# Half-size weight pieces, the second weight's extremes moved behind the first quantization, row moments by batch-norm statistics, and two halves stored from ScalarE's queue, in a block of involution and ternary convolutions

## Chip, cores and metric

One core of one Trainium2 chip. The metric is the device time of one execution in microseconds (us), as a median of runs. Data are f32; the convolutions multiply f32 data that were rounded to fp32r and their remainders.

## The reference, cut to what matters

Input x is (8, 256, 56, 56). Layer 0 is an involution on the group-normalized x, layer 1 two ternary convolutions with batch norm:

```python
x = x + involution(group_norm(x), w_reduce, b_reduce, w_span, b_span)   # K = 7, 16 groups
h = group_norm(x)
out1 = relu(batch_norm(tri_conv(h, w1)))          # 3x3, 256 -> 256
x = x + relu(out1 + batch_norm(tri_conv(out1, w2)))

def tri_conv(x, w):
    tw = w - mean(w)                              # mean of the whole weight
    lo = min(tw) + (max(tw) - min(tw)) / 3
    hi = max(tw) - (max(tw) - min(tw)) / 3
    tq = -1 where tw < lo, 1 where tw > hi, else 0
    return conv3x3(x, tq) + conv1x1(x, tq[:, :, 1, 1])
```

So each weight (256 x 256 x 3 x 3) needs its sum, maximum and minimum over all of it before any element can be made ternary, and each batch norm needs sums and sums of squares over all images before the next layer can begin.

## The kernel before, in words

**Stage 1, the involution (to about 1150 us).** An image is four quarters of 64 channels, a quarter ten rows of tiles, so the main loop (L940 to L988) has 8 x 4 x 10 = 320 rows. In a row, TensorE (PE) multiplies the row's patches with the matrices of its quarter (`apply_row`, L815), transposes the patches of later rows (L749) and makes some of the 14 units of the next quarter's matrices (`generate`, L782). VectorE (DVE) and ScalarE (ACT) move the units out of PSUM (L791, L786); ACT, DVE and GpSimd (POOL) take the result to x (`pick_out`, L827, L828, L831). POOL spreads normalized strips of x into `xn` (L674), PE transposes them (L717), ACT copies them to `stg` (L720), SyncE's queue (SP) stores them in `xtd` (L708) and loads patches `q` from there four rows ahead (L742). `params` (L557) makes the next image's group norm in steps, two a row from row 20 of each image. `pin` (L864) chains each engine's instructions in the order of the text, so in this stage every engine works in that order.

**Before the main loop** x of image 0 is loaded by halves of a quarter (L545). Then SP issues the loads of both whole weights into `wf` (L631, four DMAs of 1152 KB) and after them 16 stores of zeros from `xn` into the borders of `xtd` (L637); POOL may write `xn` only when these have read it. `extremes` (L195) takes each weight in QM = 6 pieces of 768 columns: DVE finds maximum and minimum (L208, L209), ACT the sum (L210, written over the piece itself). Nine of these 12 steps stand in the three `reduce` steps at L902 to L906 (PE's `pk`, L651; ACT's `kr`, L656), the rest in the loop over the first quarter's 14 units (L908). There too stand, for each weight, the steps that combine partitions: DVE L213 to L218, PE matmul and transpose `ends` (L222, L223), DVE L225 to L227, PE `all` (L230), DVE L232 to L245.

**Quantization** runs beside the rows from row 8, one step of the generator `quant` a row (L984). Each weight is 16 pieces of 3 x 96 columns and seven steps (rows) a piece: load into the one `piece` buffer (L257), two rows later the two comparisons (L261, L262), then L264, L273 (in half of the pieces) and L277, then L279 to L281, then L283 and L284, which leave six planes of 96 columns. The store of the planes (L287) is put into `tasks` and issued by `transfer(2)` near the head of the next row. 32 pieces make 224 rows.

**Stages 2 and 3, the convolutions** (`conv_phase`, L315): 16 halves of images, each six groups of 24 x 2 matmuls (`ORDER`, L464). From a group's results DVE makes four rows of y in turn (L484, L450). ACT takes sums and sums of squares of a half (L416, one pass each) while the next half runs (`statistics`); for the last half, `last_rows` (L420) does it row by row: rows 1 and 2 after group 4, row 0 after group 0, row 3 after group 5. Each half is stored by SP's queue, the last by ACT's (L504). `batch_norm_params` (L175) adds the columns of the statistics up (L177) and makes scale `sc` and offset `bi`, for which the next stage waits. In these stages the framework may order instructions otherwise than the text does.

**Stage 4** (L1052): loads of y1, y2, x1 (L1060), two passes each by ACT and DVE, and a store by ACT's queue (L1065).

Of the kernel before, what the change touches and what calls it, by code (L numbers as in the profile page):

```python
# [2 lines left out]

# [5 lines left out]
F32 = mybir.dt.float32  # L9
# [8 lines left out]
P = 128  # L18
# [60 lines left out]

QN, QJ = 96, 3 * C // 96
QS = WT
SLOT = (0, 2, 3, 4, 5, 1)
QM = 6


@with_exitstack
def involution_tri_block_kernel(
# [20 lines left out]
    def const_tile(shape, name):  # L110
        return const.tile(shape, F32, tag=name, name=name)
# [9 lines left out]
        for name, src in (("g1", g1), ("b1", b1), ("g2", g2), ("b2", b2)))  # L121


    st1, st2 = (const_tile([P, CT, 2, 2 * B + 2], name) for name in ("st1", "st2"))

    nc1, nc2 = (const_tile([P, CT], name) for name in ("nc1", "nc2"))
    mv2 = const_tile([P, B, NCQ, 2], "mv2")
# [62 lines left out]
        return sc, bi  # L190

    def piece_of(pool, name):
        return pool.tile([P, (4 + QS) * QN], F32, tag="piece", name=f"piece_{name}")

    def extremes(w, cols, pool, transposer, psum_tile, name):  # L195

        nf = CT * 9 * C
        n_cols = [3]

        def col(n=1):  # L200
            n_cols[0] += n
            return cols[:, n_cols[0] - n:n_cols[0]]

        s, mx, mn = col(QM), col(QM), col(QM)
        f = nf // QM
        for j in range(QM):
            v = w[:, j * f:(j + 1) * f]
            nc.vector.tensor_reduce(mx[:, j:j + 1], v, AX.X, ALU.max)  # L208
            nc.vector.tensor_reduce(mn[:, j:j + 1], v, AX.X, ALU.min)  # L209
            nc.scalar.activation(v, v, AF.Identity, accum_out=s[:, j:j + 1])  # L210
            yield
        sums, ends = col(), col(2)
        nc.vector.tensor_reduce(sums, s, AX.X, ALU.add)  # L213
        nc.vector.tensor_reduce(ends[:, 0:1], mx, AX.X, ALU.max)
        nc.vector.tensor_reduce(ends[:, 1:2], mn, AX.X, ALU.min)
        nc.vector.tensor_scalar(ends[:, 1:2], ends[:, 1:2], -1.0, None, ALU.mult)
        v = piece_of(pool, name)
        nc.vector.memset(v[:, :P], 1.0)  # L218
        yield

        ps = psum_tile(f"ends_{name}")
        nc.tensor.matmul(ps[:, P:P + 1], v[:, :P], sums, start=True, stop=True)  # L222
        nc.tensor.transpose(ps[:2, :P], ends, transposer)  # L223
        mean, top = cols[:, 0:1], col()
        nc.vector.tensor_scalar(mean, ps[:, P:P + 1], 1.0 / (P * nf), None, ALU.mult)  # L225
        nc.vector.tensor_reduce(top[:2], ps[:2, :P], AX.X, ALU.max)
        nc.vector.tensor_copy(v[:2, P:2 * P], top[:2].to_broadcast([2, P]))  # L227
        yield
        ps = psum_tile(f"all_{name}")
        nc.tensor.transpose(ps[:, :2], v[:2, P:2 * P], transposer[:2, :2])  # L230
        ex = col(2)
        nc.vector.tensor_copy(ex, ps[:, :2])  # L232
        amx, amn = ex[:, 0:1], ex[:, 1:2]

        nc.vector.tensor_tensor(amx, amx, mean, ALU.subtract)
        nc.vector.tensor_scalar(amn, amn, -1.0, mean, ALU.mult, ALU.subtract)

        d, q0, r, th = (col() for _ in range(4))
        nc.vector.tensor_tensor(d, amx, amn, ALU.subtract)
        nc.vector.tensor_scalar(q0, d, 1.0 / 3.0, None, ALU.mult)  # L240
        nc.vector.scalar_tensor_tensor(r, q0, -2.0, d, ALU.mult, ALU.add)
        nc.vector.tensor_tensor(r, r, q0, ALU.subtract)
        nc.vector.scalar_tensor_tensor(th, r, 1.0 / 3.0, q0, ALU.mult, ALU.add)
        nc.vector.tensor_tensor(cols[:, 1:2], amn, th, ALU.add)
        nc.vector.tensor_tensor(cols[:, 2:3], amx, th, ALU.subtract)  # L245
        yield

    def quantize(dst, w_dram, cols, pool, tasks, name):


        mean, lo, hi = (cols[:, k:k + 1] for k in range(3))
        for t in range(CT):
            for j in range(QJ):
                v = piece_of(pool, name)
                w, u = v[:, :3 * QN], v[:, 3 * QN:]
                o = (t * QJ + j) * 3 * QN
                nc.sync.dma_start(w, w_dram[:, o:o + 3 * QN])  # L257
                yield
                yield
                g = u[:, :3 * QN]  # L260
                nc.vector.tensor_scalar(g, w, mean, hi, ALU.subtract, ALU.is_gt)  # L261
                nc.vector.tensor_scalar(w, w, mean, lo, ALU.subtract, ALU.is_lt)  # L262
                yield
                nc.vector.tensor_tensor(g, g, w, ALU.subtract)  # L264

                def part(x, k):
                    return x[:, k * QN:(k + 1) * QN]


                c0, c1 = max(C, j * QN) - j * QN, min(2 * C, (j + 1) * QN) - j * QN  # L270
                if c0 < c1:
                    g1 = part(u, 0)[:, c0:c1]
                    nc.vector.tensor_scalar(g1, g1, 2.0, None, ALU.mult)  # L273

                e, f = part(w, 0), part(w, 1)
                g1, g0, g2 = (part(u, k) for k in range(3))
                nc.vector.tensor_tensor(e, g0, g2, ALU.add)  # L277
                yield
                nc.vector.scalar_tensor_tensor(f, g2, 4.0, g0, ALU.mult, ALU.add)  # L279
                nc.vector.tensor_tensor(part(u, 3), e, g1, ALU.add)  # L280
                nc.vector.tensor_tensor(part(u, 4), e, g1, ALU.subtract)  # L281
                yield
                nc.vector.scalar_tensor_tensor(part(u, 5), g1, 2.0, f, ALU.mult, ALU.add)  # L283
                nc.vector.scalar_tensor_tensor(part(u, 6), g1, -2.0, f, ALU.mult, ALU.add)  # L284

                def store(u=u[:, QN:], o=t * 3 * C + j * QN):
                    nc.sync.dma_start(  # L287
                        bass.AP(dst[:].tensor, dst[:].offset + o,
                                [[QS * CT * 3 * C, P], [CT * 3 * C, QS], [1, QN]]), u)

                tasks.append(store)
                yield
                yield

    def weights(i, k):

# [18 lines left out]
    def conv_phase(i, begun, src_d, norm, stats, shift, dst_d, follow):  # L315
# [104 lines left out]
        def last_rows(n, y, k0, m):  # L420

            for _ in sums(n, [y[:, to].rearrange("p (r k) -> p r k", k=4 * W)
                              [:, :, k0 * W:(k0 + m) * W] for to in range(CT)]):
                pass

        done = iter(())
        nxt, begun = {}, ({}, None)
        for _ in transform(0, raws, nxt):
# [5 lines left out]
        for n in range(2 * B):  # L434
# [22 lines left out]
            for k in ORDER:  # L457
# [34 lines left out]
                elif k == 0:  # L492
                    row_of(0, m[0], 1.5, s, ALU.add)
                    if final:
                        last_rows(n + 1, y, 0, 1)
                elif k == 5:
                    row_of(3, m[5], 6.0, d, ALU.add)
                    if final:
                        last_rows(n + 2, y, 3, 1)
                next(steps, None)  # L500
            for _ in steps:
                pass
            for to in range(CT):
                (nc.scalar if final else nc.sync).dma_start(  # L504
                    dst_d[b][to][:, h * NH:(h + 1) * NH], y[:, to])
            done = statistics(n, y)
        return begun
# [10 lines left out]
    with ExitStack() as ph1:  # L518
# [38 lines left out]
        def params(b):  # L557
# [12 lines left out]
                nc.vector.tensor_scalar(edge[:, j], dst[:, :, 1], side_sb[:, j:j + 1], None, ALU.mult)  # L570
            prm[b], prm_edge[b] = dst, edge
            yield
            ps = ps_one(f"br_{b}")
            for c in range(NCQ):
                for i in range(2):
# [46 lines left out]
        xe = [fixed([P, NX, HQ, QX], f"xe{i}") for i in range(2)]  # L622
        for v in xe:
            nc.gpsimd.memset(v, 0.0)

        nf = CT * 9 * C
        wf = apool1.tile([P, A_COLS], F32, tag="a1", name="wf")
        for i, v in enumerate((w1, w2)):
            for j in range(2):
                o = j * nf // 2  # L630
                nc.sync.dma_start(wf[:, i * nf + o:i * nf + o + nf // 2], v[:, o:o + nf // 2])  # L631
        zero = xn.rearrange("p k r x -> p (k r x)")

        for d in (d for ds in xt_d for d in ds):
            for r0, n in ((0, PAD), (PAD + HH, HQ - PAD - HH)):
                e = n * QX * RP // P
                nc.sync.dma_start(  # L637
                    bass.AP(d[:].tensor, d[:].offset + r0 * QX * RP, [[e, P], [1, e]]), zero[:, :e])

        def reduce(b, py):  # L640

# [250 lines left out]
        for _ in params(0):  # L892
            pass
        strips, around = prep(0), surround(0, 0)
        a_next = matrices(0)
        thresholds = [pieces.tile([P, 32], F32, tag=f"cols{i}", name=f"cols{i}") for i in range(2)]
        ext = [extremes(wf[:, i * nf:(i + 1) * nf], thresholds[i], pieces, ident_sb, ps_one, f"w{i}")
               for i in range(2)]

        found = chain(*(islice(v, QM) for v in ext), *ext)  # L900

        for py in range(PY):  # L902
            next(strips)
            transfer(len(tasks))
            reduce(0, py)
            for _ in range(3):  # L906
                next(found)
        for u, _ in enumerate(generate(0, 0, a_next)):  # L908
            if u < 4 or u % 3 == 0 and u < 12:
# [23 lines left out]
        for k in rows[:QLEAD]:  # L933
            transpose_q(*k)
        pin()
        norm = iter(())
        quant = chain(*(quantize(wq_d[i], v, thresholds[i], pieces, tasks, f"w{i + 1}")
                        for i, v in enumerate((w1, w2))))
        last = None
        for m, (b, c) in enumerate(quarters):  # L940
            a = a_next
# [195 lines left out]
```

## Time and profile before

| | |
|---|---|
| time, median of 3 runs | 2258.8 us (2254.0, 2258.8, 2258.85) |
| the profiled execution's own time | 2269.48 us |
| its span | 2267.7 us |
| granted TensorE clock, mean | 0.924 |
| busy, share of the span | PE 82%, PE weight loads 76%, DVE 75%, ACT 56%, POOL 26% |

Busy times of the stages, from the windows of that execution (us):

| window | what | PE | DVE | ACT | DMA share |
|---|---|---|---|---|---|
| 0 to 24 | loads of x, first group norm | 1.72 | 11.68 | 1.49 | 0.88 |
| 24 to 47 | `reduce` steps and extremes | 17.41 | 16.16 | 9.40 | 0.49 |
| 47 to 79 | the first quarter's units | 24.03 | 20.23 | 15.70 | 0.33 |
| 1156 to 1585 | first convolution | 428.71 | 407.02 | 278.76 | 0.36 |
| 1585 to 1601 | to the second | 0.29 | 10.85 | 8.97 | 0.71 |
| 1601 to 2030 | second convolution | 428.02 | 406.71 | 282.05 | 0.34 |

A line of the timeline reads: start and length in us, engine, line, operation, out<-in with their shapes, xcount, and in brackets how long the engine sat idle before it and what ended that. A line of the windows: the window, its length, then the busy time (and count) of PE, PEld, DVE, ACT and POOL, then the granted clock, the DMA share and GB/s. A group's line that has three durations with slashes gives the shortest, median and longest in ns. In the waits, each line has the sum, the number and the longest wait in us. The span's 40 slices have about 56.7 us each.

### The profile page before, as it was taken

How to read it: one execution, taken by the hardware profiler on the slowest of the kernel's cores; microseconds unless marked ns; L12 is line 12 of the kernel's file. 1: busy time of each engine (PE TensorE's matmuls, PEld its weight loads, DVE VectorE, ACT ScalarE, POOL GpSimd, SP SyncE). 2: the span in 40 equal slices, each digit the busy share in tenths (PEclk: the TensorE clock that was granted, in tenths of full speed). 3: DMA queues.
4: the chain of work that ended last, by engine and by line, in shares of the span. 5: the costliest groups of instructions: out<-in, count | busy, mean ns of one | idle time of the engine just before them, and what ended most of it. 6: DMA issues, size and time to landing. Idle time of an engine off the chain costs nothing.

```text
span 2267.7 us, 72706 instructions
## 1 busy us (share of the span) xinstructions
PE 1866.4 (82%) x31088; PEld 1716.6 (76%) x31088; DVE 1706.7 (75%) x2906; ACT 1268.3 (56%) x2461; POOL 584.5 (26%) x1320
## 2 busy tenths in 40 slices
PE   4889899898998989999879999999799999970000
PEld 3778777777877877778779999999799999970000
DVE  6676857667585775655689999998999999975444
ACT  3555455455554645556446766665576666673434
POOL 2545546364563645546400000000000000000000
PEclk9899999999999999999989999999899999995555
DMA  6556646566474754645453333334333333369999
GB/s 211 154 157 181 199 131 206 147 192 189 131 221 120 225 164 138 197 119 160 138 206 116 129 134 140 119 116 161 133 138 117 116 116 116 116 255 401 410 430 403
DMA packets 156447, 411.24 MB, mean 181 GB/s; under 512 B 51550, under 2 KB 62172, under 8 KB 148444
## 3 DMA queue, kind: packets, MB, share of 16 engines
q1 hardware_dynamic: 150528, 376.56, 49.9%
q10 hardware_dynamic: 5596, 30.03, 3.2%
q8 instruction: 245, 4.01, 0.8%
q14 instruction: 78, 0.64, 0.1%
HBM read 264.05 MB, written 142.48 MB: 179 GB/s over the span
## 4 chain that ended last, share of the span: by engine, by line
PE 38%; DMA 7%; DVE 3%; ACT 1%; issue 1%; ACTq 0%; SPq 0%; POOL 0%; DVEq 0%
PE c L464 37%; DMA y1f<-y1d 3%; DMA x1f<-x1d 2%; DMA out_y<-x1f 1%; DVE x1f L1064 1%; DMA y2f<-y2d 1%; ACT dummy L416 1%; DVE y1f L1062 0%; ACT y1f L1061 0%; ACT y1f L1063 0%; PE pa L815 0%; PE ptq L749 0%; DVE q L346 0%; DVE r L366 0%; DVE u L373 0%
## 5 line engine op out<-in xcount | busy, mean ns | idle before, releaser
L464 PE MATMUL c<-pl,wq 128*128 128x392 f32 x4608 | 857.1, 348 | 20.2 <-ACT pl L351 20.2
L464 PEld LDWEIGHTS c<-pl,wq 128*128 128x128 f32 x4608 | 855.1, 189 | 22.0 <-ACT pl L351 20.7
L791 DVE TENSOR_TENSOR a<-pg,bt 126x756 f32<-126x756 f32 (+3 forms) x640 | 393.2, 656 | 192.7 <-ACT a L786 147.3
L782 PE MATMUL pg<-kr,wl 64*126 64x140 f32 (+1 forms) x6144 | 459.4, 294 | 14.3 <-DVE a L791 7.1
L782 PEld LDWEIGHTS pg<-kr,wl 64*126 64x126 f32 x6144 | 396.8, 196 | 66.4 <-issue 41.5
L815 PE MATMUL pa<-a,q 126*32 126x48 f32 x17920 | 273.2, 208 | 62.3 <-issue 38.5
L815 PEld LDWEIGHTS pa<-a,q 126*32 126x32 f32 x17920 | 223.1, 111 | 115.8 <-issue 53.4
L786 ACT ACTIVATE a<-pg,bt 126x126 f32<-126x126 f32 x768 | 243.3, 475 | 102.6 <-PE pg L782 102.4
L831 POOL TENSOR_TENSOR x<-x,inv 128x168 f32<-128x168 f32 x320 | 166.4, 520 | 438.5 <-DVE inv L828 375.5
L828 DVE SCALAR_TENSOR_TENSOR inv<-pa,half_sb,inv 128x168 f32<-128x168 f32 x320 | 117.1, 366 | 171.0 <-ACT inv L827 144.8
L351 ACT CAST pl<-r 128x812 fp32r<-128x812 f32 x192 | 162.5, 868 | 145.2 <-DVE r L346 126.9
L752 ACT COPY q<-ptq 126x384 f32<-126x384 f32 x320 | 138.2, 481 | 162.7 <-issue 96.2
L331 POOL MEMSET xp<- 128x116 f32 x32 | 6.3, 195 | 829.4 <-DVE a L346 829.4
L416 ACT ACTIVATE dummy<-y,nc 128x1568 f32<-128x1568 f32 (+2 forms) x144 | 210.1, 1459 | 5.3 <-DVE y L484 3.5
L674 POOL TENSOR_SCALAR xn<-x,gn 128x224 f32<-128x224 f32 (+2 forms) x384 | 179.1, 486 | 130.0 <-PE pt L717 70.8
L352 DVE TENSOR_TENSOR pl<-r,pl 128x812 fp32r<-128x812 f32 x192 | 187.2, 1002 | 28.2 <-ACT pl L351 27.0
L674 POOL TENSOR_SCALAR xe<-x,gn 128x168 f32<-128x168 f32 (+2 forms) x384 | 161.2, 439 | 0.0
L720 ACT COPY stg<-pt 98x512 f32<-98x512 f32 x128 | 74.9, 585 | 137.0 <-issue 88.5
L749 PE MATMUL ptq<-ident_sb,xe 128*126 128x128 f32 x960 | 144.2, 285 | 4.6 <-DVE var_a L170 2.6
L150 DVE BATCH_NORM_STATS2 st<-x 128x6 f32<-128x392 f32 x256 | 138.3, 557 | 11.8 <-DMA x<-in_x 10.2
L827 ACT ACTIVATE inv<-pa,half_sb 128x168 f32<-128x168 f32 x320 | 128.2, 401 | 26.8 <-PE pa L815 25.7
L1011 ACT ACTIVATE xp<-raw,gn 128x392 f32<-128x392 f32 (+1 forms) x124 | 82.6, 721 | 62.9 <-DVE a L346 58.9
(144 smaller groups left out, 1846.2 us busy)
## 6 DMA issues: line engine op xcount, KB each, us to landing
q<-xtd SPq DMA_DIRECT2D x320, 252.0 KB
raw<-x1d SPq DMA_DIRECT2D x32, 812.0 KB
raw<-y1d SPq DMA_DIRECT2D x32, 812.0 KB
x<-in_x SPq DMA_DIRECT2D x64, 392.0 KB
xtd<-stg SPq DMA_DIRECT2D x128, 196.0 KB
x1d<-x SPq DMA_DIRECT2D x64, 392.0 KB
y1d<-y SPq DMA_DIRECT2D x30, 784.0 KB
y2d<-y SPq DMA_DIRECT2D x30, 784.0 KB
```

What stands on the lines that cost most here:

```text
L150: nc.vector.bn_stats(st[:, j, :], xt[:, j * NC:(j + 1) * NC])
L351: nc.scalar.copy(hi, r)
L352: nc.vector.tensor_tensor(lo, r, hi.bitcast(F32), ALU.subtract)
L416: nc.scalar.activation(dst, v, f, bias=shift[:, to:to + 1], accum_out=stats[:, to, j, n:n + 1])
L464: nc.tensor.matmul(ps[:, to, :NM], wq[k][:, t, dx, to * P:(to + 1) * P], part[:, t, :, dx:dx + W], start=(c == 0), stop=(c == last))
L674: nc.gpsimd.tensor_scalar(dst[:, i - d - k0:f - d - k0, :, x0:x0 + n], v[:, i:f, :, j0:j0 + n], scale, bias, ALU.mult, ALU.add)
L749: nc.tensor.transpose(pt[:NQ, k * P:(k + 1) * P], xe[c % 2][:, k, PY * ty:PY * ty + QY].rearrange("p r x -> p (r x)"), ident_sb)
L782: nc.tensor.matmul(dst, wl[rows, c, gp, o:o + NQ], kr[py][rows, px, :], start=True, stop=True)
L786: nc.scalar.activation(whole[:, g0 + i, p0 + j], ps[:NQ, i, j * nt:(j + 1) * nt], AF.Identity, bias=bt[:, c, g0 + i, p0 + j:p0 + j + 1])
L791: nc.vector.tensor_tensor(dst[:, g0:g0 + 2, p0:p0 + nv].rearrange("q g p t -> q g t p"), ps[:NQ, :, t0 * nv:t1 * nv].rearrange("q i (t p) ...
L815: nc.tensor.matmul(ps[o:o + 32, k * 2 * n:(k + 1) * 2 * n], q[:NQ, k, o:o + 32], av[:, t + k, g * 2 * n:(g + 1) * 2 * n], start=True, stop ...
L831: nc.gpsimd.tensor_tensor(xv, xv, iv.rearrange("p t (y x) -> p y t x", x=PX), ALU.add)
```

## The change

- `QN` is 48 instead of 96: a quantized piece has 3 x 48 columns, there are 32 for each weight, the `piece` tile has half the size and two buffers. The steps stand in a table of events now (`paced`): two half pieces in seven rows; comparisons, L264, L273 and L277 in one row (`ternary`), the other five operations in the next (`planes_of`), and the store three rows after those, issued where its step stands and no longer through `tasks`. The load of the next piece in that buffer stands one row after the store.
- Only w1 is loaded whole, and after the zeros. Its six pieces are two a `reduce` step, its combining steps in units 0 to 2.
- w2's extremes are a part of `quant`, between the two quantizations: 12 pieces of 384 columns from the `piece` buffers, two in five rows, with maximum, minimum and sum all by DVE. There is a row more between some of its combining steps.
- `quant` has 115 + 36 + 115 = 266 steps instead of 224.
- `params` has one empty step before the matmuls `br` (L576).
- Last half of a convolution: rows 0 and 3 go through `bn_stats` on DVE, are aggregated and turned into sums of the two rows together, instead of eight passes by ACT. The statistics have one column less.
- The last two halves (n >= 2B - 2) are stored by ACT's queue, not only the last.

```diff
-QN, QJ = 96, 3 * C // 96
+QN, QJ = 48, 3 * C // 48
-QM = 6
+QM, QM2 = 6, 12
...
-        return pool.tile([P, (4 + QS) * QN], F32, tag="piece", name=f"piece_{name}")
+        return pool.tile([P, (4 + QS) * QN], F32, tag="piece", bufs=2, name=f"piece_{name}")
...
+        def fetch(j):
+            held[j] = piece_of(pool, name)[:, :f]
+            nc.sync.dma_start(held[j], w_dram[:, j * f:(j + 1) * f])
+        def seek(j):
+            v = w[:, j * f:(j + 1) * f] if w is not None else held[j]
             nc.vector.tensor_reduce(mx[:, j:j + 1], v, AX.X, ALU.max)
             nc.vector.tensor_reduce(mn[:, j:j + 1], v, AX.X, ALU.min)
-            nc.scalar.activation(v, v, AF.Identity, accum_out=s[:, j:j + 1])
-            yield
+            if w is not None:
+                nc.scalar.activation(v, v, AF.Identity, accum_out=s[:, j:j + 1])
+        def add(j):
+            nc.vector.tensor_reduce(s[:, j:j + 1], held.pop(j), AX.X, ALU.add)
...
+                r = 5 * (j // 2) + j % 2 * 2
+                events.setdefault(r, []).append(lambda j=j: fetch(j))
+                events.setdefault(r + 2, []).append(lambda j=j: seek(j))
+                events.setdefault(r + 3, []).append(lambda j=j: add(j))
...
+        for k in range(CT * QJ):
+            r = 7 * (k // 2) + k % 2 * 3
+            for n, f in ((0, fetch), (2, ternary), (3, planes_of), (6, store)):
+                events.setdefault(r + n, []).append(lambda f=f, k=k: f(k))
...
+        def row_stats(st, y, k, j):
+            for to in range(CT):
+                v = y[:, to].rearrange("p (r k) -> p r k", k=4 * W)[:, :, k * W:(k + 1) * W]
+                nc.vector.bn_stats(st[:, to, j], v)
+        def row_sums(n, st):
+            mv = st[:, :, 2, :2]
+            for to in range(CT):
+                nc.vector.bn_aggr(mv[:, to, :], st[:, to, :2].rearrange("p n s -> p (n s)"))
+            sq = st[:, :, 2, 2]
+            nc.vector.tensor_tensor(mv[:, :, 0], mv[:, :, 0], shift, ALU.add)
+            nc.vector.tensor_tensor(sq, mv[:, :, 0], mv[:, :, 0], ALU.mult)
+            nc.vector.tensor_tensor(mv[:, :, 1], mv[:, :, 1], sq, ALU.add)
+            nc.vector.tensor_scalar(stats[:, :, :, n], mv, 2.0 * HT * W, None, ALU.mult)
...
-                        last_rows(n + 1, y, 0, 1)
+                        row_stats(moments, y, 0, 0)
...
-                        last_rows(n + 2, y, 3, 1)
+                        row_stats(moments, y, 3, 1)
+                        row_sums(n + 1, moments)
...
-                (nc.scalar if final else nc.sync).dma_start(
+                (nc.scalar if n >= 2 * B - 2 else nc.sync).dma_start(
...
             prm[b], prm_edge[b] = dst, edge
             yield
+            yield
             ps = ps_one(f"br_{b}")
...
-        for i, v in enumerate((w1, w2)):
-            for j in range(2):
-                o = j * nf // 2
-                nc.sync.dma_start(wf[:, i * nf + o:i * nf + o + nf // 2], v[:, o:o + nf // 2])
...
+        for j in range(2):
+            o = j * nf // 2
+            nc.sync.dma_start(wf[:, o:o + nf // 2], w1[:, o:o + nf // 2])
...
-            for _ in range(3):
+            for _ in range(2):
                 next(found)
...
-        quant = chain(*(quantize(wq_d[i], v, thresholds[i], pieces, tasks, f"w{i + 1}")
-                        for i, v in enumerate((w1, w2))))
+        made = [quantize(wq_d[i], v, thresholds[i], pieces, f"w{i + 1}")
+                for i, v in enumerate((w1, w2))]
+        quant = chain(made[0], ext[1], made[1])
```

The last two loads of `wf` in the diff stand after the loop of the zeros' stores (L634 to L638), which is unchanged itself.

## The prediction

> **What bounds the kernel now.** I read the page's 40 slices first, then the windows, then the timeline at each seam.
>
> ```profile
> PE   4889899898998989999879999999799999970000
> DVE  6676857667585775655689999998999999975444
> DMA  6556646566474754645453333334333333369999
> 79.00:1150.00 1071.00, 965.54 (x26128) 826.56 (x26126) 714.65 (x1697) 572.92 (x1568) 556.04 (x1237) 0.97 0.59 169
> 2030.00:2268.00 238.00, 0.00 (x0) 0.00 (x0) 113.42 (x55) 97.92 (x59) 0.00 (x0) 0.51 0.98 410
> ```
>
> The involution's rows are 90% PE (965.54 of 1071) and 67% DVE; the convolutions are PE alone (the table above); the last 238 us are DMA alone (share 0.98). So the change can win or lose in three kinds of place: the first 79 us, where PE is busy 43 us, the seams before the second convolution and the last stage, and as added load in the rows.
>
> ```profile
> 35.59 1.34 POOL L674 TENSOR_SCALAR xn<-x,gn 128x224 f32<-128x224 f32 x3 [31.85 <-DMA xtd<-xn]
> 36.98 1.09 PE L717 MATMUL pt<-ident_sb,xn 128*98 128x128 f32 x4 [5.59 <-POOL xn L674]
> 67.74 0.43 PE L222 MATMUL ends_w<-cols,piece_w 128*128 128x1 f32 x2 [1.51 <-DVE piece_w L218]
> PE ends_w L222 <- DVE piece_w L218: 4.8, 2, 3.3
> ```
>
> In the brackets: POOL waits for the zeros' stores, PE 5.59 us for POOL. The waits' line says that PE later waits 4.8 us in two pieces for the extremes' combination.
>
> **1. The start.** SP issues its first `wf` load at 12.02 and the zeros from 17.27 to 33.38; their last packet lands at 34.87, POOL starts 0.72 later. In the change the zeros take the places of the loads: the first eight at the moments 12.02 to 22.66, the other eight at the 0.47 us pitch of the last ten, so the last at 26.4. Landing (34.87 - 33.38 = 1.5) and POOL's 0.72 give 28.6, and PE can transpose 1.39 after that, at 30.0. PE's `pk` group (24.41 + 6.98) ends at 31.4, so PE goes straight on: the 5.59 us of idle time are gone, and I take 5.5.
>
> What is late next is w1. Its halves are issued at 26.9 and 27.3. All four loads together took 12.5 us (packets from 16.55 to 29.02), 3.1 each, so the halves land near 31 and 34. DVE's twelve L208 and L209 start 0.86 apart in the timeline: 31 to 36.2, then 36.2 to 41.4. ACT's last L210 comes after the third `kr` and ends near 44.3; with L213 to L218 (0.9) `ends` is ready at 45.2. PE's first unit now starts at 47.27 and would at 41.8; `ends` stands after the second, near 45.5. So it just fits. Of the 4.79 us of waits for `ends` (3.28 and 1.51) one weight's remains, without w2's six L210 and six DVE reductions ahead of it; I leave it 0.8, so 4.0 go. POOL's pace of strips (2.2 us a unit at 50 to 55) stays. Sum: **-9.5 us**. Bounds: -3 (w1 lands 4 us late and `ends` is waited for, but the first gap is shut) to -13 (the clock, half speed for 13.6 us between 44.8 and 85.8 in the trace, stays up too).
>
> **2. More DVE work beside the rows.** Median durations:
>
> ```profile
> L261 DVE TENSOR_SCALAR piece_w<-piece_w,cols x32: 414/423/804, 114.2 to 860.5; 128x288 f32<-128x288 f32 x32
> L277 DVE TENSOR_TENSOR piece_w<-piece_w x32: 243/255/473, 118.1 to 868.3; 128x96 f32<-128x96 f32 x32
> L208 DVE TENSOR_REDUCE cols<-wf x12: 943/956/969, 24.6 to 54.5; 128x1 f32<-128x768 f32 x12
> ```
>
> Three shapes, nearly a line: (423 - 255) / 192 = 0.88 ns an element, on 170 ns that no size takes away. So 144 elements are about 0.30, 48 about 0.21, 384 about 0.53 us. A piece now is three of 0.42 to 0.45, six of 0.25 and half an L273 (0.21): 2.9 us. A half piece is 3 x 0.30 + 6 x 0.21 + 0.07 = 2.25, two 4.5. Neighbours overlap (L283 and L284 start 0.17 apart for 0.25 each), so of the 1.6 us more I count 1.1; x 32 = 35 us. w2's 36 reductions: 0.5 x 36 = 18, and 2 for its small steps. **DVE gets 55 us more** between rows 8 and 273.
>
> What of it reaches PE? The rows answer. Images 1 to 4 (from the start of each image's first L827) took 138.3, 137.9, 137.9 and 136.8 us with 16.0, 17.2, 16.7 and 15.7 us of quantization on DVE; image 6, which has none, 135.2. That is 2.5 us for 16.4 of work, 15%. Without PE's own long stops (over 0.5 us, "issue" in the waits: 7.0, 9.3, 5.0, 5.6 against 5.4) it is 131.0 against 129.8, 1.2 us or 7.6%. I take 8%: **+4.5 us**; bounds 0 and 15% (8.3), and the rival below for more. The cover is DVE's idle third; where a row has none left, L828 and L791 are late, and PE waits for PSUM.
>
> The Trainium skill speaks against this part: "VectorE: DVE Perf Modes", section on the TRN2 errata, says that vector operations out of SBUF pay a fixed price per instruction and advises tiles of at least 512 elements; its formula (N + 151) / 0.96 ns gives 207 ns for 48 elements, like the line through this trace's rows. Taken as time on the path the rule would make all of the 55 us a loss; the row of image 6 says that a small part is.
>
> **3. Queues in the rows.** Loads and stores of pieces double from 64 to 128, and w2 adds 12: at L257's 0.37 and L287's 0.56 us of issue, 64 x 0.47 + 12 x 0.37 = 34 us of SP's time, spread over 266 rows of 3.4. On the other side SP now stands 95 us in 27 waits (3.5 each, SP's own waits from 200 to 1000 us) for DVE before L287, with the `q` loads queued behind; three rows later that wait is gone. The load that refills a buffer follows its store by one row instead of nearly two: stores landed in 3.2 us (median of the 32, first issue to last packet), so SP may wait some 1 to 2 us there, and behind it only the `q` load for four rows on. ACT waited for such a load once in rows 200 to 1000 us (2.4 us). Both ends, nothing and one such wait in twenty rows (13 x 0.5 = 6 us), stand; I take 0. The extra steps around w2's `ends` put a row between DVE and PE, so no wait there. The empty step in `params` moves `br` past `pick_out`, which has no PE instruction: PE's order stays, its 1.8 us wait for `gn` stays. 0.
>
> The planes' packets go from 384 to 192 B. In this trace those of 384 B took 24 ns each (mean, 200 to 860 us); 49,152 packets at even that price are 74 us on each of 16 engines in some 900, 37 more than now, at a share of 0.6: hidden. The Trainium skill ("DMA: Bandwidth & Descriptors", the table that opens it) asks for 512 B or more in a transfer for line rate, which both sizes miss; no row here shows the price of 192 B.
>
> **4. The seams.**
>
> ```profile
> 1584.75 1.04 DVE L450 SCALAR_TENSOR_TENSOR y<-c,d 128x392 f32<-128x392 f32 x2 [1.44 <-PE c L464]
> 1590.29 0.23 DVE L177 TENSOR_REDUCE bmv_bn<-st 128x4 f32<-128x72 f32 x1 [4.50 <-ACT dummy L416]
> 2037.35 0.23 DVE L177 TENSOR_REDUCE bmv_bn<-st 128x4 f32<-128x72 f32 x1 [7.25 <-ACT dummy L416]
> SPq L1060 <- DVE pl L352: 0.7, 1, 0.7
> ```
>
> L177 waits for ACT, which works off eight passes of 0.75 us. They go. DVE adds, after y at 1585.8: two `bn_stats` (1.03 a pair, L150), two aggregations (at most 0.27, L555), four small operations (0.19): 1588.1. Row 0's two fit DVE's 1.44 us wait for PE. **-2.2 us**, all of it on the path, since PE waits for `bi`. Before the last stage the same gives 2032.4 instead of 2037.35, -4.9. But DMA runs at share 1.01 from 2014 to 2043 on loads already issued; earlier scales only close the dip at 2042 to 2046 (0.96, 370 GB/s against 425): **-0.7 us**; bounds 0 and -4.9. The store moved to ACT's queue frees SP at 1990, but the next loads wait for L352's end at 2013.95 (last line above), 1 us after that store was issued. ACT pays 0.7 us in a stretch where it idles 2 us (2018 to 2020). 0.
>
> **Sum**: -9.5 + 4.5 - 2.2 - 0.7 = -7.9 on an execution of 2269.48 us, 10.7 above the median of the runs. On the median 2258.8 that is 2250.9.
>
> **Rivals.** (a) DVE's slack gives out: from rows 8 to 273 half pieces put 1.2 us of DVE work into one row (`ternary`, where 0.86 was the most), ahead of the next L828. For it: DVE is at 69% in the rows from 200 to 900 us. Against: the 8%. From 23% on it eats the whole gain of 12.4; at 50% it is 27.5 - 12.4 = +15: 2274. (b) The start keeps only 3 to 5 us, since w1, now behind the zeros, holds `ends` and ACT: -4 + 4.5 - 2.9 = -2.4: 2256. (c) The seam at 2037 counts in full, and PE's clock stays up at the start: -13 + 4.5 - 2.2 - 4.9 = -15.6: 2243. (d) ScalarE's queue and the `params` step do nothing: in the sum already.
>
> **Numbers.** About 0.3% (6.8 us) is what can be told from no change: 2252.0 and 2265.6. Forecast (2245 to 2256) 50%, of which some 30 points lie under 2252; (b) 20%, a few points of it under; (c) 15%; (a) 15%, most of it over 2265.6. So faster 0.48, same 0.39, slower 0.13. Range 2240 to 2268, which reaches into (c) and (a).
>
> **What would show it.** L717's first wait gone and the first L782 near 42; first L827 near 73 instead of 82.7; L177 near 2 and 5 us after the last L450. Images 1 to 6 within 1 to 2 us of 137.7 and DVE's share up by 5 points; longer images, with PE waiting for L791, would make it wrong, as would a first L827 later than 78.

## The result and the profile after

The changed kernel takes **2255.6 us** (median of 20 runs, 2248.6 to 2259.5), the kernel before 2258.6 beside it (20 runs, 2248.4 to 2269.8): a ratio of 0.9976, interval 0.9963 to 0.9988. The forecast was 2250.9 within 2240 to 2268. The total is near it; the terms are not. The start gained twice what was forecast and the rows lost three times as much. The profile below is of the shortest of the 20 executions, 2248.59 us; that of the kernel before, 2269.48 us, was 11 us over its median.

The same three lines of the 40 slices, now of the changed kernel (span 2246.8 us, against 2267.7):

```profile
PE   5989898998989989899889999998899999970000
DVE  6767868678686876856599999998999999984444
DMA  6647658476474756746453333335333333369999
```

PE's first slices are fuller and DVE's share in the rows is up; after the first 20 slices no digit differs by more than one. Now the start. The windows of the kernel before (window and length; busy time and count of PE, PEld, DVE, ACT, POOL; granted clock; DMA share; GB/s):

```profile
33.80:40.60 6.80, 3.62 (x16) 2.61 (x18) 6.37 (x8) 1.58 (x5) 2.67 (x6) 0.50 0.20 65
47.00:79.00 32.00, 24.03 (x230) 19.79 (x229) 20.23 (x60) 15.70 (x43) 15.14 (x36) 0.79 0.33 100
```

The same windows of the changed kernel:

```profile
33.80:40.60 6.80, 6.80 (x70) 5.69 (x68) 6.80 (x9) 6.23 (x14) 1.65 (x4) 1.00 0.21 65
47.00:79.00 32.00, 28.68 (x644) 24.42 (x642) 18.96 (x34) 18.21 (x53) 20.54 (x49) 1.00 0.60 172
```

The granted clock was 0.50 and 0.79 and is 1.00. The timeline of the changed kernel there:

```profile
12.54 10.87 SPq L691 DMA_DIRECT2D xtd<-xn  x16
23.45 0.92 SPq L698 DMA_DIRECT2D wf<-in_w  x2
25.22 1.34 POOL L734 TENSOR_SCALAR xn<-x,gn 128x224 f32<-128x224 f32 x3 [21.47 <-DVE brn L640]
30.41 0.64 PE L777 MATMUL pt<-ident_sb,xn 128*98 128x128 f32 x4
38.66 0.88 PE L842 MATMUL pg<-kr,wl 64*126 64x140 f32 x12
42.16 0.28 PE L254 MATMUL ends_w<-cols,piece_w 128*128 128x1 f32 x2
```

POOL no longer waits for a DMA, and PE's first transpose and the matmul for `ends` have no bracket: they wait for nothing. The first row of the involution (first `inv` on ACT, L827 before and L887 now) begins at 64.3 us instead of 82.7. The waits of PE and SP between 80 and 1150 us in the kernel before (sum, number, longest):

```profile
PE pg L782 <- DVE a L791: 6.0, 12, 1.7
PE br L576 <- DVE gn L173: 10.9, 7, 1.6
SPq L287 <- DVE st L150: 49.1, 17, 4.4
SPq L257 <- DMA wqd<-piece_w: 31.1, 20, 3.4
```

and between 62 and 1130 us in the changed kernel:

```profile
PE pg L842 <- DVE a L851: 12.4, 17, 2.1
PE br L637 <- DVE gn L173: 11.1, 7, 1.6
PE pg L842 <- DVE piece_w L315: 4.9, 6, 1.3
PE pk L711 <- DVE piece_w L315: 1.8, 3, 0.6
SPq L294 <- DMA wqd<-piece_w: 90.6, 48, 4.4
```

PE now waits for the quantization itself (`piece_w`, 6.7 us, before 0.3); `br` waits as before (10.9 us in seven). SP's wait has moved: before the stores it stands for DVE 28 us instead of 104 in all (L287 before, whose largest group is shown), before the refill of a buffer three times as long (L257 before, L294 now). At the two seams:

```profile
1565.18 1.04 DVE L507 SCALAR_TENSOR_TENSOR y<-c,d 128x392 f32<-128x392 f32 x2 [0.45 <-PE c L521]
1568.31 0.23 DVE L177 TENSOR_REDUCE bmv_bn<-st 128x4 f32<-128x68 f32 x1
2013.42 0.22 DVE L177 TENSOR_REDUCE bmv_bn<-st 128x4 f32<-128x68 f32 x1 [2.10 <-ACT dummy L456]
```

L177 no longer waits at the first seam, and 2.10 instead of 7.25 us at the second.

### The profile page after: what moved, and what is told of

The parts are those of the page before. It is cut to its first block, busy times and chain, and to the rows that moved or that the text cites. A ratio compares the mean times of both kernels' runs of the same rounds, so it can differ in the third digit from the quotient of the medians.

```text
span 2246.8 us, 73149 instructions
## 1 busy us (share of the span) xinstructions
PE 1853.7 (83%) x31088; PEld 1706.2 (76%) x31088; DVE 1756.9 (78%) x3246; ACT 1251.7 (56%) x2417; POOL 579.6 (26%) x1320
## 4 chain that ended last, share of the span: by engine, by line
PE 71%; DVE 11%; DMA 8%; issue 4%; ACT 3%; POOL 0%; SPq 0%; DVEq 0%; ACTq 0%; POOLq 0%
PE c L521 38%; PE pg L842 14%; PE pa L875 8%; PE ptq L809 4%; DVE a L851 4%; PE pk L711 3%; DMA y1f<-y1d 2%; PE pt L777 2%; DMA x1f<-x1d 2%; DMA y2f<-y2d 2%; ACT a L846 2%; DVE x1f L1124 1%; DVE st L150 1%; DVE inv L888 1%; DMA q<-xtd 1%
## 5 line engine op out<-in xcount | busy, mean ns | idle before, releaser
L842 PE MATMUL pg<-kr,wl 64*126 64x140 f32 (+1 forms) x6144 | 449.4, 290 | 23.2 <-DVE a L851 14.6
L842 PEld LDWEIGHTS pg<-kr,wl 64*126 64x126 f32 x6144 | 387.2, 192 | 74.4 <-issue 41.4
L456 ACT ACTIVATE dummy<-y,nc 128x1568 f32<-128x1568 f32 (+1 forms) x128 | 200.2, 1564 | 2.1 <-ACT pl L391 0.8
L887 ACT ACTIVATE inv<-pa,half_sb 128x168 f32<-128x168 f32 x320 | 128.2, 401 | 26.4 <-PE pa L875 21.2
L1122 DVE SCALAR_TENSOR_TENSOR y1f<-y2f,sc_bn,y1f 128x3136 f32<-128x3136 f32 (+2 forms) x20 | 56.6, 2831 | 81.5 <-ACT y1f L1121 43.8
```

Of the source, the lines that this page charges most:

```text
L456: nc.scalar.activation(dst, v, f, bias=shift[:, to:to + 1], accum_out=stats[:, to, j, n:n + 1])
L842: nc.tensor.matmul(dst, wl[rows, c, gp, o:o + NQ], kr[py][rows, px, :], start=True, stop=True)
```

## The theories and the experiments

**Theory.** The start gains 18 us in every execution, because PE's stops and the half clock that goes with them are gone; the rows give most of it back, because half pieces cost DVE more operations (and SP more issues), and more of that reaches PE than the forecast's 8%. **Rivals:** the start's gain belongs to one execution; the order of the zeros alone makes it; the rows' loss is w2's extremes, or the DMAs of half pieces, or only a difference between two executions.

All stages in one table. Start: to the first `inv`. Rows: from `inv` 8 to `inv` 274. DVE and half clock: DVE's busy time, and the time at half clock, in those rows. The ratio is to the kernel before, timed beside it, and is worked out from all runs, as is the median; the columns behind it are of one profiled execution each.

| kernel | median us | ratio, interval | start | rows | DVE | half clock | first seam |
|---|---|---|---|---|---|---|---|
| before | 2258.6 | 1 | 82.7 | 917.7 | 622.8 | 51 | 16.00 |
| after | 2255.6 | 0.9976 (0.9963 to 0.9988) | 64.3 | 921.5 | 679.8 | 44 | 13.58 |
| b_again | 2253.7 | 0.9992 (0.9971 to 1.0013) | 83.9 | 907.1 | 622.0 | 44 | 16.00 |
| a_again | 2246.7 | 0.9965 (0.9942 to 0.9987) | 64.5 | 924.3 | 678.8 | 61 | 13.58 |
| s_zeros | 2250.0 | 0.9979 (0.9957 to 1.0) | 79.1 | 905.7 | 622.1 | 31 | 16.00 |
| a_zeros_last | 2245.8 | 0.9962 (0.9941 to 0.9984) | 65.6 | 923.3 | 678.2 | 51 | 13.58 |
| a_dve3 | 2294.5 | 1.0177 (1.0143 to 1.0211) | 64.7 | 968.7 | 764.6 | 61 | 13.58 |
| a_noext | 2241.2 | 0.9949 (0.9933 to 0.9965) | 64.7 | 917.3 | 660.9 | 38 | 13.59 |
| a_pool | 2234.7 | 0.9919 (0.9895 to 0.9942) | 64.7 | 912.9 | 634.8 | 41 | 13.59 |
| a_spread | 2243.0 | 0.9941 (0.9916 to 0.9966) | 64.6 | 912.4 | 676.7 | 48 | 13.58 |
| a_split | 2242.9 | 0.9939 (0.9917 to 0.996) | 64.9 | 919.3 | 638.1 | 56 | 13.59 |
| a_whole | 2232.0 | 0.9905 (0.988 to 0.9929) | 65.5 | 904.2 | 638.1 | 27 | 13.59 |
| a_best | 2236.7 | 0.9916 (0.9885 to 0.9947) | 64.8 | 920.1 | 637.5 | 65 | 13.58 |
| a_sums | 2258.5 | 1.0022 (1.0005 to 1.0038) | 65.6 | 926.8 | 679.7 | 48 | 18.49 |

### Both kernels once more: b_again, a_again

No edit.

> The kernel of before unchanged, profiled a second time. Theory A (the start is worth 18 us in every execution, and the rows give back what the medians lack): its first L827 stands near 82.7 us again, and rows, convolutions and last stage have the lengths of the first profile within 2 us. Theory B (the first profile of before was a long one: PE's clock was at half speed in the start): the first L827 stands at 72 to 78 us, with fewer half-speed windows before 90 us, and the whole execution is 5 to 10 us shorter than 2269.48. Time against the kernel before: 0, within 0.3%.

> The changed kernel unchanged, profiled a second time. Theory A: first L827 near 64.3 us again, the 320 rows 1062 to 1064 us, and the time 18 us under before in its profile. Theory B: first L827 at 64 to 68 us, the rows or the last stage longer than in the first profile by 3 to 8 us. Both expect the measured time 3 to 8 us under the kernel before.

The start's gain comes back (83.9 against 64.5), as theory A has it. What A expected of the rows did not come: all 320 took 1049.7 us in b_again and 1064.3 in the first profile, not the same within 2 us. The rows' loss shows even so: 917.7, 907.1 and 905.7 us with the old pieces (s_zeros is the third), 921.5, 924.3, 923.3 and 926.8 with the new (a_zeros_last and a_sums are the last two): on average 910.2 against 924.0, **13.8 us** for 57 us more of DVE work. Two things bound this figure. The four executions stood 51 us at half clock on average and the three 42, which is worth some 4 to 5 us (an estimate: half of the 9 us). And the ratios hold it up: start and seams gained some 22 us, while 0.9976, 0.9965 and 0.9962 (a_zeros_last, whose start is 1.2 us longer) are gains of 5 to 9 us, so 12 to 17 were lost elsewhere. The profile of the kernel before on which the forecast rests was a long draw: its rows are 10 to 12 us longer than in the other two executions with the same pieces. Laid beside the changed kernel's own profile (921.5), it hides most of the loss.

### Only the order of the zeros: s_zeros and a_zeros_last

s_zeros is the kernel before with the loads of `wf`, all four, behind the zeros; a_zeros_last is the changed kernel with w1's two loads in front of them again.

```diff
+        (the two loads of w1 into wf)
         for d in (d for ds in xt_d for d in ds):
             (the zeros' stores)
-        (the two loads of w1 into wf)
```

> The kernel of before with one edit: the loop of zero stores stands ahead of the loads of both whole weights. My reckoning of the start (step 1): PE's 5.59 us wait for POOL's strip goes, the last zero lands near 25 us and the first L717 follows the first reduce group without a gap; the later waits for ends stay (3 to 5 us in all), so the first L827 comes 4 to 7 us earlier than in the profile of before of the same call. Rival: the four weight loads, now last, land so late (near 40 us) that ACT's L210 and DVE's L208 hold kr and the units, and the first L827 is no more than 2 us earlier.

> The change with the sixteen zero stores issued behind w1's two loads, as the kernel before has it, and all else as in the change. The theory that the start gained twice, by PE's gap itself and by the half clock that follows gaps, expects the first wait of PE for xn back with 3 to 5 us, a stretch at half clock after it, and 70 to 75 us from the start to the first inv where the change has 64.5. If the half clock came from the second weight's extremes alone, the clock stays whole and the start takes 64.5 plus the gap less what w1's earlier landing saves: 66 to 69.

The order is worth little either way: 3.6 to 4.7 us in the kernel before, about 1.2 in the changed one (65.6 us, just under the rival's 66 to 69). In a_zeros_last the first transpose waits only this long:

```profile
31.67 0.64 PE L776 MATMUL pt<-ident_sb,xn 128*98 128x128 f32 x4 [1.42 <-POOL xn L733]
```

The zeros go out by 28.2 us although w1 goes first, because w2's two loads are no longer in front of them. And s_zeros, which has the first gap closed, still shows the clock down a little later, in these windows:

```profile
24.00:47.00 23.00, 19.93 (x160) 15.32 (x160) 19.05 (x31) 13.32 (x28) 6.54 (x15) 1.00 0.61 234
47.00:79.00 32.00, 25.23 (x258) 21.03 (x260) 19.72 (x59) 13.92 (x39) 12.61 (x31) 0.68 0.31 94
```

Its PE waits 2.39 and 1.51 us for `ends` and about 1 us for several units, as the kernel before does. So the expectation that the gap and the half clock would return in a_zeros_last fell: **taking w2 out of the start** makes most of the 18.5 us, and the order the rest.

### More DVE work in the same rows: a_dve3

```diff
+            for _ in range(3):
                 (the five operations of planes_of)
```

> The changed kernel with the five operations of planes_of made three times each (same results), so VectorE has 640 operations of 48 columns more, about 80 us of work, in rows 8 to 273. Step 2's share of 8% gives +6 us, the upper bound of 15% gives +12; the rival (a), slack gone, gives 50% or more, +40.

86 us more of DVE work (764.6 against 679 in the rows) made the kernel 47.8 us slower than a_again, timed beside it, 56%, and the rows some 45 us longer: what rival (a) had at 50%. PE's largest wait in the rows of a_dve3:

```profile
PE pg L843 <- DVE a L852: 52.9, 54, 2.2
PE pa L876 <- DVE a L852: 17.3, 21, 1.3
```

The first line was 12.4 us in 17 waits in the changed kernel and 6.0 in 12 in the kernel before. The price climbs: 24% for the first 57 us (13.8 of 57, whatever the doubled DMAs cost included), over half for the next 86. DVE is busy over 90% of the time in 60 of the 266 rows before, in 98 after, in 145 here. That fits rows which run out of idle DVE time and pass the rest on; it is not shown row by row, and a_spread below has 98 such rows too, with rows that are 12 us shorter than the mean of 924.0.

### Whole pieces, with all else: a_whole

```diff
-QN, QJ = 48, 3 * C // 48
+QN, QJ = 96, 3 * C // 96
-QM, QM2 = 6, 12
+QM, QM2 = 6, 6
-tag="piece", bufs=2
+tag="piece", bufs=1
```

With it the seven steps of a piece and its store are laid out as in the kernel before, and w2's extremes come in six pieces of 768 columns, each five rows apart.

> The changed kernel with whole pieces again: 96 columns, one buffer, the operations of a piece over four rows as before the change, w2's extremes still beside the rows (six pieces of 768 columns, five rows each). Theory D (the rows lengthen by what VectorE has more to do): VectorE's busy time from row 8 to row 274 falls from 680 to about 640 us and the 266 rows from 923 to 914 us; time 8 us under the changed kernel. Theory E (the rows lengthen by SP's waits before the refills of the buffers): with one buffer these waits stay, and the rows stay within 3 us of 923.

Rows of 904.2 us, the shortest of all, with w2's extremes among them, and 2232.0 us, more than theory D's 914 us and 8 us: **half pieces, with their two buffers and their work in two rows, cost 0.6 to 0.7%, about 15 us** (0.9905 against 0.9965 and 0.9976), and w2's extremes, as whole pieces, nothing that shows: start and seams alone gained some 22 us, and 0.9905 is 21.4. This kernel beats both.

### Without w2's extremes: a_noext

```diff
-        made = [quantize(wq_d[i], v, thresholds[i], pieces, f"w{i + 1}")
+        made = [quantize(wq_d[i], v, thresholds[0], pieces, f"w{i + 1}")
                 for i, v in enumerate((w1, w2))]
-        quant = chain(made[0], ext[1], made[1])
+        quant = chain(made[0], made[1])
```

> The changed kernel without w2's extremes: that part of the computation is left out, and w2 is quantized with w1's mean and bounds. 36 rows are without added work and quantization ends in row 238. Theory D: 20 us less work on VectorE at 22%, so the 266 rows are 4 to 5 us shorter, 918. Rival: the extremes are a third or more of the 13 us that the rows lost, since their matmuls and PSUM tiles stand in PE's order; then 8 us or more.

19 us less of DVE work (and 12 loads) make the rows 6.7 us shorter than the mean of 924.0, and the time 0.9949. By the ratios that is 4 to 6 us under the change, and the intervals overlap. So with half pieces around them the extremes may cost up to a third of their length; beside whole pieces no cost shows. The 6.7 us are not all theirs for sure: this execution stood 38 us at half clock, the four others 51 on average.

### DVE's sum, its lumps, or the DMAs: a_pool, a_spread, a_split

a_pool keeps the half pieces and their DMAs, moves five of the operations of a half piece to POOL (the doubling of `g1` as an addition), spreads the rest over three rows and lets ACT make w2's sums. a_spread keeps all of DVE's work, over four rows instead of two. a_split has whole pieces, each loaded and stored by two DMAs:

```diff
-            nc.sync.dma_start(v[:, :3 * QN], w_dram[:, k * 3 * QN:(k + 1) * 3 * QN])
+            n = 3 * QN // 2
+            for h in range(2):
+                o = k * 3 * QN + h * n
+                nc.sync.dma_start(v[:, h * n:(h + 1) * n], w_dram[:, o:o + n])
```

> The changed kernel with five of the ten operations of a half piece on GpSimd (the subtraction of the comparisons, the doubling, e, and planes 3 and 4), a row later, and the sums of w2's pieces on ScalarE. Loads and stores are the same in number and size. Theory D: VectorE's busy time from row 8 to row 274 falls from 680 to about 620 us, the level of before, and the 266 rows to about 911; time 10 to 14 us under the changed kernel, 16 to 20 under before. Theory E (the queues): no change in the rows. Rival: GpSimd, half busy, hands its strips and its sums over later, and the rows are longer.

> The change with the half pieces' operations laid over four steps again (comparisons, ternary, five planes, the last two planes; the store three rows after the ternary step's row at the earliest), where the change puts them into two. DVE's sum in the rows stays at 680 us; the most that falls into one row goes from about 1.2 us to about 0.7. If the loss of the rows comes from the sum of DVE's work: rows 8 to 274 near 922 us and the time of the change. If it comes from the lump in one row: near 910 us, and 8 to 12 us under the change.

> Whole pieces as in a_whole (quantization of w2, its extremes, DVE's work all as there), but each load and each store of a piece is issued as two DMAs, so that the rows have as many issues and as many stored packets of 192 bytes as the change. It tells queues and packets apart from DVE's work. If the rows' loss is DVE's work (theory D): rows 8 to 274 stay at 904 us, give or take 4, and the time is a_whole's, 0.990 of the kernel before. If it is the issues on SP's queue or the small packets (theory E): 910 to 914 us there and a time 5 to 10 us over a_whole's.

- a_pool gets most of the 15 us back (0.9919) with the change's DMAs left as they are. That speaks for DVE.
- a_split loses 8 to 10 us to a_whole (0.9939 against 0.9905), with DVE's work unchanged. That speaks for the DMAs, and for more than a_pool leaves for them; a_split issues its pairs back to back, which the change does not. Against a_best (below), whole pieces too and timed beside it, the loss is only 5 to 6 us, and the intervals overlap either way.
- a_spread's rows are as short as expected of the lump (912.4), but its profiled execution, 2235.1 us, was 7.9 under its own median; by the medians it is 3 us under a_zeros_last, timed beside it, and the intervals overlap.

So that half pieces cost 15 us is shown, and a_pool shows that DVE's work, its sum or its place in the rows, is a part of it. **How the 15 us divide among DVE's sum, its lumps and the doubled DMAs stays open**: the parts differ by less than the intervals.

### ACT's sums again, store on ACT's queue: a_sums

```diff
-                        moments = half("s2") ... row_stats(moments, y, 0, 0)
+                        last_rows(n + 1, y, 0, 1)
-                        row_stats(moments, y, 3, 1); row_sums(n + 1, moments)
+                        last_rows(n + 2, y, 3, 1)
```

> The changed kernel with the last half's rows 0 and 3 summed by ScalarE again (the code of before). Step 4: the seam between the convolutions is 16.0 us instead of 13.6, and the last stage 0 to 1 us longer; time 2 to 3.5 us over the changed kernel. Rival (c): the last stage is 4 to 5 us longer.

The seam is not 16.0 us, as before the change, but 18.49, and the last stage took 241.8 us, 3.3 to 4.0 more than in the changed kernel's two profiles, so rival (c) came close to what happened. The time ratio is 1.0022, 10 to 13 us over the changed kernel; the first seam and the last stage make some 8 of them. L177 of a_sums:

```profile
1582.23 0.23 DVE L177 TENSOR_REDUCE bmv_bn<-st 128x4 f32<-128x72 f32 x1 [6.97 <-ACT dummy L456]
```

ACT is late by 2.5 us more, and the reason stands in the changed kernel too, at the copy `e` of the last half:

```profile
1556.34 0.81 ACT L531 COPY e<-c 128x784 f32<-128x784 f32 x1 [5.22 <-PE c L521]
```

ACT idles 5.22 us before it and works off three of the four passes over half 14 afterwards, from 1557.05 to 1562.2. With that half's store on SP's queue (a_best) three run before the copy and one after it:

```profile
1557.50 0.81 ACT L540 COPY e<-c 128x784 f32<-128x784 f32 x1 [2.20 <-PE c L530]
```

So moving the store to ACT's queue reorders ACT's passes and costs ACT some 2.5 us (18.49 against 16.00, where ACT ends the seam). At the first seam the moments on DVE hide it: the seam ends by DVE, and is 13.58 in a_best as well. At the second they do not. There L177 waits 2.10 us for ACT in the changed kernel, and in a_best for nothing:

```profile
2012.26 0.22 DVE L177 TENSOR_REDUCE bmv_bn<-st 128x4 f32<-128x68 f32 x1
```

It starts 3.16 us after PE's end instead of 5.16, and the last stage of a_best took 235.0 us, where every other kernel with the moments on DVE took 237.2 to 240.0. In this one profile the store on ACT's queue thus costs 2 us or more.

### The waits of br as well: a_best

```diff
             yield
             yield
+            yield
             ps = ps_one(f"br_{b}")
...
-                (nc.scalar if n >= 2 * B - 2 else nc.sync).dma_start(
+                (nc.scalar if final else nc.sync).dma_start(
```

This on top of a_whole.

> a_whole (whole pieces, all else as in the change) with two edits. One more empty step ahead of br in params, so that br stands a row later in PE's order, behind more of PE's work that does not need gn: the waits of br for gn, 1.6 us in each of seven images, should go, 8 to 11 us off the rows. And half 14's store back on SP's queue, so that ACT's passes of that half are not behind it: the first seam 13.6 us or less. Together 8 to 11 us under a_whole, 0.986 of the kernel before. If br's wait is only moved to what stands behind it, the rows stay at a_whole's 1046 us and the time at 0.990.

Not so: 2236.7 us, 0.9916, no different from a_whole. Its rows of 920.1 us are of an execution that was 9 us over its own median. PE's waits in the rows of a_whole:

```profile
PE br L646 <- DVE gn L173: 11.5, 7, 1.6
PE pg L851 <- DVE a L860: 9.1, 17, 2.1
```

and of a_best:

```profile
PE pg L852 <- DVE a L861: 24.5, 20, 2.4
```

The wait of `br` is gone, and PE stops as long a few matmuls later: while DVE works through the chain that makes `gn`, it moves no unit out of PSUM (at the image whose wait ends at 543.12, none from 537.99 to 542.18). So it is the time that DVE takes for this chain that holds PE up, more than the place of `br`.

## Why the prediction was right, and where its steps failed

**Step 1, the start, -9.5 forecast, -18.4 in the two profiles (-17 to -20 among all with either start).** The mechanism was right: the 5.59 us gap and the waits for `ends` (4.79) went, a little more than was counted. The mis-sized term is the clock, which stood only in the bound of -13. The first `pk` group took 5.92 instead of 6.98 us (its matmuls go from one pair in 0.46 us to one in 0.23 at 28.4 us instead of 30.4), the second 3.67 instead of 4.95, and from the first `pg` to the first `inv` passed 25.7 us instead of 35.5, twice what `ends` explains. The forecast also misread the clock's records, which are counted from 11.0 us earlier than the span: on the span half speed lasted from 33.8 to 40.6, 57.7 to 64.5 and 67.9 to 74.7, three times 6.8 us and 20.5 in all, not 13.6, each beginning in or shortly after one of PE's waits. The waits that were to go and the slow stretches were one term, not two. And the step gave the order of the zeros the credit for the gap; in a_zeros_last, with the old order, w2's loads gone leave 1.42 us of the 5.59. w1's halves, thought to be what is late next, were not: `ends` is waited for nowhere.

**Step 2, DVE beside the rows, +4.5 forecast, +13.8 measured (step 3's part, put at 0, included).** DVE's 55 us were right (57). The share was wrong: not 8% but up to 24%, over the upper bound of 15%. The 8% came from a difference of 1.2 us between images of one execution, while the rows of one kernel differ by 10 to 12 us between executions, 1.5 us an image; a difference that small could not carry the step. The same difference, images 1 to 4 less image 6, which was 2.5 us there, is 1.8 in b_again and 7.5 in s_zeros, with the same pieces. And it was read at old pieces of at most 0.86 us a row, then used for half pieces that put 1.2 us into one row. Rival (a) named this mechanism and the 23% from which it takes all of the forecast's gain; the rows did reach it, and the start's unforeseen half paid. The slope was not the same for all operations either: the comparisons took 0.35 us at 144 elements where the line gives 0.30.

**Step 3, queues, 0 forecast.** The empty step in `params` does nothing, as forecast (11.1 us of waits against 10.9). SP's waits moved to the refill, 90.6 us in 48 or 1.9 each, also as forecast; of those before the stores, said to go, 28 of 104 us stayed. Whether the doubled DMAs cost nothing is open: a_split says 5 to 10 us for pairs issued together, a_pool at most a few for the change's own.

**Step 4, the seams.** First seam 16.00 to 13.58, -2.4, forecast -2.2. Second: from PE's end to L177 8.32 to 5.16, -3.2 where -4.9 was forecast, since ACT's earlier passes now end last (2.10 us); the last stage went from 238.7, 238.6 and 239.8 us to 238.5 and 237.8, by about the forecast 0.7. That ACT pays 0.7 us for the store, in idle time, was too low: some 2.5 us, hidden at the first seam, while at the second it is the 2.10 us for which L177 still waits. The store's term of 0 was wrong by some 2 us, if a_best's one profile is typical.

**The sum.** -18.4 + 13.8 - 2.4 - 0.8 = -7.8, beside the forecast's -7.9, with both large terms mis-sized by 9 us in opposite directions: that the sum came out so near was luck. The ratios of the two times that the changed kernel was timed, 0.9976 and 0.9965, are 5 and 8 us. The two tests that the forecast set itself in the rows, images 1 to 6 within 1 to 2 us of 137.7 (135.2 to 140.3, four of the six within 2, their mean 137.8) and 5 points more of DVE's share (66.8% to 72.2%), were met about as written and showed nothing, since the profile that they were set against was a long one.

## What to carry to other kernels

Before small terms are read from one profile, find out how far two executions of the same kernel lie apart in that stage. Count a stop of PE together with the slow clock that can follow it. Work hidden on a second engine has no fixed price: look how many rows have little idle time left on it, and cut a task into pieces only if the fixed time of the added operations and DMAs still fits there.

## What the runs showed of the hardware

- PE's clock fell to half in stretches of 3.4 us and multiples of it, which lie on one grid of 3.41 us steps within an execution, and stops much shorter than a step went ahead of them: in a_whole six of the eight stretches in rows 8 to 274 follow within some 2 us on the 1.6 us wait of `br`, once an image. Counted over the steps at full clock in all 14 profiles, up to 1120 us: where PE was busy for less than half of a step, the next was at half speed in 108 of 109 cases; from half to 70%, in 77 of 431; above 70%, in none of 3686. The Trainium skill ("TensorE: Matmul & The Clock Gate", Part 1) describes free-running windows of about 3.4 us, which agrees, and advises against idle gaps above 3.4 us; here waits of 1.5 and 3.3 us already went with 6.8 us at half speed each.
- The time at half clock in rows 8 to 274 varied from 27 to 65 us between executions, from 44 to 61 for the changed kernel alone, and the longer rows mostly go with it (a_whole 904.2 with 27, a_split 919.3 with 56, a_best 920.1 with 65, at equal DVE work). A part of the reason is where a stop falls on the grid: in the 13 profiles that have it, the 1.6 us wait of `br` was followed by half speed all 47 times that it lay within one step, and 27 of the 39 times that it lay across two.
- On DVE an operation of two tensors took 0.20 us on 128 x 48 elements, 0.25 on 128 x 96 and 0.31 on 128 x 144, and the reductions 0.54 on 128 x 384: the line that the forecast drew, with 0.17 us fixed, gives 0.21, 0.25, 0.30 and 0.51. The comparisons do not lie on it: 0.35 us on 128 x 144 and 0.42 on 128 x 288, so their fixed part is nearer 0.27 (an estimate from these two).
